# Graph network over 128 graphs: x turned by DMA and VectorE, the odd-weight check on other engines, and a new order of steps

## The chip, the cores and the metric

The kernel runs on one core of one Trainium2 chip. A core has five engines that run their own instruction streams in order and wait for each other by semaphores: TensorE (PE; its weight loads are shown apart as PEld), VectorE (DVE), ScalarE (ACT), GpSimd (POOL) and SyncE (SP), which issues nearly all DMAs of this kernel. The metric is the device time of one execution in microseconds; the profile shows one execution of the program.

## The reference

There are 128 graphs of 64 nodes with 128 features (x), and a 0/1 adjacency matrix for each (adj), symmetric and with ones on the diagonal; about an eighth of the entries are ones. For each pair of nodes a message is computed and the messages of the neighbours are added up:

```python
pair_feats = concatenate([f_i, f_j], axis=-1)
messages = _mlp(pair_feats, msg_w0, ...) * coupling_matrix[..., None]
agg = sum(messages, axis=2)
updated = part_feats + _mlp(concatenate([part_feats, agg], axis=-1), upd_w0, ...)
# _mlp: relu(x @ w0 + b0), layer norm, relu(h @ w1 + b1), layer norm, h @ w2 + b2
```

All of it is float32.

## The kernel before, in words

The kernel computes messages for existing edges alone. Graphs go in pairs (64 pairs, one graph on partitions 0 to 63 and one on 64 to 127), four pairs make a block (`PB = 4`, 16 blocks, `NB`), and each graph has room for `CAP = 640` edges, so a pair has 10 tiles of 128 edges, and a chunk is four tiles: 160 chunks, ten to a block.

For each block, ahead of its chunks: `load_adj` and `load_x` bring the adjacency (`an`, 128 KB) and x (`xn`, 256 KB) by SP's queue. `rank` (L729) is a VectorE scan along the adjacency's rows that numbers each row's edges; `count` (L738) is a small matmul, and `place` and `place_out` on GpSimd turn the counts into edge positions (`posall`). `odd_weights` (L805) checks on VectorE that every adjacency entry is 0 or 1: it forms (a - 1) * a and takes the largest absolute value into `nball`. At the very end `flag_in` reads `nball`; if anything is odd, a dense path computes everything instead. With these inputs it is not taken. `turn_x` (L813) transposes the block's four 128x128 tiles of x on TensorE into a PSUM bank (`ma`), and `turn_x_out` (L819) copies them to `xnT` on ScalarE. `rows_both` multiplies `xnT` by the two halves of w0; `rows_hi` and `rows_lo` split the products into a high and a low part (`abh`, `abl`) in the type that `gather` multiplies.

For each pair: `distance` (ScalarE) and `make_tp` (VectorE) build a 0/1 matrix `tp` that says which edge slot belongs to which row node; `node_rows` casts it to `i` on GpSimd, `marks` (TensorE) and `compare` (VectorE) make `j` for the column node, and `stack` copies parts of both into `S` by SP's DMAs (`s<-i`, `s<-j`). `node_marks` turns `tp` by a DMA transpose (`oh`).

For each chunk: `gather` multiplies S by abl and abh into PSUM (`hps`), `relu0` (ScalarE) makes `h`, `turn_h` transposes it on TensorE into the one `hT` bank so that `stats0` (VectorE) can take the layer norm's statistics, `layer1` multiplies h by w1 (`z`), `relu1` (ScalarE or VectorE) makes `y`, and `stats1` takes its statistics. `weights` (GpSimd) and `reduce` (TensorE) add the messages up, and a `Unit` of steps per block runs the update network and ends in `finish`, four VectorE operations and the DMA to the output.

What sets the order is a list: each step is entered by `at(n, tag, fn, ...)` with a number of the chunk and gets the time `144 * n + t`, where `t` comes from the table `WHEN`, by the step's name and its place. The steps are then sorted by this time and emitted one after another, which gives each engine's order. The scheduler of the framework is off in this part (`manual_schedule`); it only adds the semaphores. A step's number is a rank in a list and no time on the chip.

`keep_busy` is filler: matmuls of constants whose results nobody reads, at the start.

Of the kernel before, what the change touches and what calls it, by code (L numbers as in the profile page):

```python
# [49 lines left out]
    "count": {8: -202, 101: 130, 102: 110, 115: -196},  # L50
    "count.0": {100: 66},
    "count_out": {9: -224, 101: 56, 102: 96, 115: -273},
    "count_out.0": {100: 79},
    "degrees": {9: -369, 101: -144, 102: -4, 115: -419},
    "degrees.0": {100: 58},
    "distance": {0: -532, 3: 185, 5: -470, 8: -359, 103: 34, 104: 302, 105: -163, 106: 312,
        107: -610, 108: 189, 158: -893, 159: -639, 160: -591, 161: -589, 162: 13, 163: -1137},
    "distance.0": {100: 163},
    "distance.1": {101: 208},
    "distance.2": {102: 283},  # L60
    "empties.0": {100: 156},
    "empties.1": {100: 154},
    "empties.10": {100: -158},
    "empties.11": {100: 84},
# [42 lines left out]
    "inverse_of": {0: -218, 5: 125, 125: -319, 126: -100, 127: 107, 128: 421, 129: 168, 130: 263,  # L107
# [1549 lines left out]
```

## Time and profile before

| | |
|---|---|
| time, median of 3 runs | 496.4 us (495.78 to 496.48) |
| span of the profiled execution | 495.0 us |
| TensorE busy | 484.8 us (98%) |
| VectorE busy | 462.3 us (93%) |
| ScalarE busy | 397.9 us (80%) |
| GpSimd busy | 353.0 us (71%) |
| mean busy share of the DMA engines on SP's queue | 60.4% |

A busy time is the union of an engine's instructions. Matmul ends are modelled, so distances between starts tell more of TensorE than lengths. In a list of groups, each row has the line, the engine, the operation, what it writes and reads, the count, then the total busy time, the mean of one in ns, and the idle time before it. Rows of a timeline start with the start and the length in microseconds.

### The profile page before, as it was taken

To read this page: it belongs to the slowest core of one execution; us is meant where nothing else is said; L and a number is where in the kernel's file an instruction comes from. 1 tells how busy PE (TensorE), PEld (TensorE's weight loads), DVE (VectorE), ACT (ScalarE), POOL (GpSimd) and SP (SyncE) were. 2 spreads that over 40 slices of the span, in tenths; PEclk is the share of its full clock that TensorE was granted. 3 is DMA by queue.
4 is the path that set the end of the run, shared out by engine and by line. 5 is a ranking of instruction groups with operands and counts; after the bars stand their busy time and mean duration, and the time that the engine had idled before them with its cause. 6 is when DMAs were issued, how large, how long until landed. Compare 5 with 4: busy or idle time off the path is not lost.

```text
span 495.0 us, 15915 instructions
## 1 busy us (share of the span) xinstructions
PE 484.8 (98%) x5947; PEld 461.3 (93%) x5947; DVE 462.3 (93%) x1225; ACT 397.9 (80%) x907; POOL 353.0 (71%) x563
## 2 busy tenths in 40 slices
PE   7999999999999999999999999999999999999994
PEld 5798999999999999999999999999999999999994
DVE  7989989999999999999999999999999999989975
ACT  7999978888787887878878787887878778767753
POOL 3276768878778787777779777787877678576661
PEclk9999999999999999999999999999999999999998
DMA  4676685667656575765757657466956775564311
GB/s 123 140 176 150 135 142 120 129 139 152 143 121 140 117 155 130 154 137 114 147 109 164 130 134 158 110 139 130 170 126 115 161 102 132 134 102 107 61 39 47
DMA packets 91474, 63.55 MB, mean 128 GB/s; under 512 B 57473, under 2 KB 75522, under 8 KB 91394
## 3 DMA queue, kind: packets, MB, share of 16 engines
q1 hardware_dynamic: 91106, 62.36, 60.4%
q8 instruction: 49, 0.80, 0.7%
q14 instruction: 31, 0.25, 0.1%
q10 hardware_dynamic: 288, 0.13, 0.1%
HBM read 7.15 MB, written 4.19 MB: 23 GB/s over the span
## 4 chain that ended last, share of the span: by engine, by line


## 5 line engine op out<-in xcount | busy, mean ns | idle before, releaser
L984 PE MATMUL z<-w1c,h 128*128 128x128 f32 x1280 | 190.0, 275 | 0.0
L984 PEld LDWEIGHTS z<-w1c,h 128*128 128x128 f32 x1280 | 171.7, 191 | 3.9 <-issue 0.4
L936 ACT ACTIVATE h<-hps,b0c 128x512 f32<-128x512 f32 x160 | 109.0, 681 | 42.3 <-PE hps L931 40.7
L627 DVE BATCH_NORM_STATS2 st<-hT 128x6 f32<-128x256 f32 x320 | 122.2, 418 | 15.3 <-PE hT L941 12.7
L627 DVE BATCH_NORM_STATS2 st<-y 128x6 f32<-128x256 f32 x320 | 125.3, 419 | 0.0
L978 ACT ACTIVATE z<-b1b,m_sd 128x128 f32<-128x128 f32 x320 | 118.4, 371 | 6.5
L941 PE MATMUL hT<-ident,h 128*128 128x128 f32 x640 | 113.3, 276 | 0.2 <-DVE st L627 0.2
L931 PE MATMUL hps<-s,abl 128*128 128x512 f32 (+3 forms) x256 | 97.0, 381 | 0.6 <-DVE abl L865 0.3
L971 POOL TENSOR_TENSOR u<-b1b,m_sd 128x512 f32<-128x512 f32 x80 | 87.5, 1103 | 7.8 <-ACT m_sd L635 7.7
L931 PE MATMUL hps<-s,abh 128*128 128x512 f32 (+3 forms) x256 | 92.2, 365 | 0.0
L941 PEld LDWEIGHTS hT<-ident,h 128*128 128x128 f32 x640 | 77.2, 141 | 2.9 <-PE z L984 0.6
L1027 POOL TENSOR_TENSOR w<-oh,m_q 128x192 f32<-128x192 f16 x126 | 65.2, 533 | 17.2 <-DVE m_q L656 9.6
L914 DVE TENSOR_TENSOR j<-mk,cmpt 128x320 fp32r<-128x320 f32 x124 | 59.3, 478 | 2.8 <-PE mk L906 1.2
L995 ACT ACTIVATE y<-z 128x512 f32<-128x512 f32 x80 | 47.9, 598 | 17.3 <-PE z L984 17.0
L611 DVE CUSTOM_DVE_ANT_0 y<-z,u 128x512 f32<-128x512 f32 x80 | 54.2, 678 | 1.7 <-PE z L984 0.2
L931 PEld LDWEIGHTS hps<-s,abl 128*128 128x128 f32 x256 | 48.8, 191 | 5.2 <-ACT ab L851 2.0
L889 POOL CAST i<-tp 128x640 fp32r<-128x640 f16 x58 | 41.8, 721 | 16.6 <-DMA s<-i 11.5
L874 ACT ACTIVATE d<-slot,mid 128x640 f16<-128x640 f16 x64 | 52.4, 822 | 0.4 <-DVE tp L880 0.3
L931 PEld LDWEIGHTS hps<-s,abh 128*128 128x128 f32 x256 | 49.5, 193 | 0.2
L645 POOL TENSOR_TENSOR m_v<-m_v,st 128x20 f32<-128x20 f32 x31 | 7.2, 232 | 57.5 <-DVE st L627 54.6
L1042 PE MATMUL ys<-y,w 128*32 128x128 f32 x1488 | 44.1, 274 | 0.0
L1042 PEld LDWEIGHTS ys<-y,w 128*32 128x32 f32 x1488 | 39.6, 110 | 2.6 <-issue 1.7
(193 smaller groups left out, 883.2 us busy)
## 6 DMA issues: line engine op xcount, KB each, us to landing
s<-j SPq DMA_DIRECT2D x124, 160.0 KB, 2.8
s<-i SPq DMA_DIRECT2D x124, 160.0 KB, 2.7
xn<-in_x_dram SPq DMA_DIRECT2D x15, 256.0 KB, 3.6
out_dram<-uo SPq DMA_DIRECT2D x15, 256.0 KB, 2.5
an<-in_adj_dram SPq DMA_DIRECT2D x16, 128.0 KB, 3.9
oh<-tp SPq DMA_TRANSPOSE x64, 3.5
xn<-in_x_dram SPq DMA_DIRECT2D x2, 128.0 KB, 2.9
out_dram<-uo SPq DMA_DIRECT2D x2, 128.0 KB, 3.9
```

Of the source, the lines that this page charges most:

```text
L611: nc.vector._custom_dve(TENSOR_ADD_SAT, out=o, in0=ps, in1=sb, s0=BIG, s1=0.0)
L627: nc.vector.bn_stats(st, src.rearrange("p t c -> p c t"))
L874: nc.scalar.activation(D[p], slot, AF.Abs, bias=blocks[b]["mid"][:, q:q + 1], scale=-1.0)
L914: nc.vector.tensor_tensor(JR[p][:, c], MK.pop((p, k))[:, 0:HC], cmpt[:, c], op=ALU.is_equal)
L931: nc.tensor.matmul(HP[n][:, c:c + w], lhsT=blocks[g // (2 * PB)]["ab", g // 4 % 2][k][:, g % 4, :], rhs=S[g // 2][:, g % 2, e:e + w], star ...
L936: nc.scalar.activation(H[n], HP.pop(n), AF.Relu, bias=b0c)
L941: nc.tensor.transpose(HT[n][:, t, :], H[n][:, t * P:(t + 1) * P], ident)
L971: nc.gpsimd.tensor_tensor(U[n], bc(W["b1b"], CH), SR[q][:, k:k + CH].unsqueeze(2).to_broadcast([P, CH, C]), op=ALU.mult)
L978: nc.scalar.activation(z_of(n)[:, t, :], W["b1b"], AF.Copy, scale=SR[q][:, k:k + 1])
L984: nc.tensor.matmul(ps[:, t, :], lhsT=H[n][:, t * P:(t + 1) * P], rhs=W["w1c"], start=by_vector(n) and t == 0, stop=True, skip_group_check= ...
L1027: (nc.vector if p == NP - 2 else nc.gpsimd).tensor_tensor(WT[p][:, g], oh, qs, op=ALU.mult)
L1042: nc.tensor.matmul(YS[b][g * N + m * HN:g * N + (m + 1) * HN, k, :], lhsT=w[:, g, m, u, :], rhs=y, start=(u == 0), stop=(u == TH - 1), til ...
```

## The change

It does four things.

1. For blocks 2 to 15, x is loaded a second time, straight from HBM, by four DMAs on SP's queue (`load_xt`). Each writes 32 partitions. Partition 32c + b gets, for every 32-row group k of the block's 512 rows, the 32 numbers of row 32k + b and columns 32c to 32c + 31, a run of 128 bytes. VectorE's transpose, which turns each 32x32 square of its input by itself, then gives `xnT` at once (`swap_x`). The four TensorE transposes and ScalarE's copy of these blocks go. Blocks 0 and 1 stay as they were. The first load of x stays too, for the residual.
2. `odd_weights` computes a - 1 and then (a - 1) * a on GpSimd, and a new step `odd_sum` lets ScalarE add up the absolute values of the row. The sum is compared with 0 as the maximum was.
3. `WHEN` is replaced as a whole, so all steps stand in a new order.
4. Some small things follow from the order: tiles are no longer dropped from the tables by the step that happened to come last, and `S`, `usdb` and the statistics are made by whichever step comes first.

```diff
-    "load_adj": {1: -901, 102: -1519, 103: 320},
-    "rank": {6: -172, 101: 62, 102: -12},
-    "turn_x": {6: -532, 101: -146, 115: -480},
+    "load_adj": {1: 1034, 102: 1731, 103: 755},
+    "load_xt": {2: 613, 102: 827, 115: 1278},
+    "rank": {6: 397, 101: -593, 102: 1209},
+    "swap_x": {7: 256, 115: 2738},
+    "turn_x": {101: 1025},
...
+        def load_xt(b):
+
+            xp = blocks[b]["xp"] = blkp.tile([P, PB * P // 32, 32], F32, name="xp", bufs=1)
+            rows = xf[b * PB * P:(b + 1) * PB * P, :].rearrange("(k b) c -> b k c", b=32)
+            for c in range(C // 32):
+                nc.sync.dma_start(xp[c * 32:(c + 1) * 32], rows[:, :, c * 32:(c + 1) * 32])
+
+        def swap_x(b):
+
+            blk = blocks[b]
+            blk["xnT"] = blkp.tile([P, PB * P], F32, name="xnT", bufs=4)
+            nc.vector.transpose(blk["xnT"], blk.pop("xp").rearrange("p k a -> p (k a)"))
...
         def odd_weights(b):
 
             an = blocks[b]["an"]
-            a2 = adp.tile([P, PB, N], F32, name="a2")
-            nc.vector.scalar_tensor_tensor(a2, an, 1.0, an, op0=ALU.subtract, op1=ALU.mult)
-            nc.vector.tensor_reduce(nball[:, b:b + 1], a2.rearrange("p q j -> p (q j)"),
-                                    axis=AX.X, op=ALU.max, apply_absolute_value=True)
+            a2 = blocks[b]["a2"] = adp.tile([P, PB, N], F32, name="a2", bufs=1)
+            nc.gpsimd.tensor_scalar(a2, an, 1.0, None, op0=ALU.subtract)
+            nc.gpsimd.tensor_tensor(a2, a2, an, op=ALU.mult)
+
+        def odd_sum(b):
+
+            a2 = blocks[b].pop("a2").rearrange("p q j -> p (q j)")
+            nc.scalar.activation(a2, a2, AF.Abs, accum_out=nball[:, b:b + 1])
...
                 at(max(o - 7, 13), "", odd_weights, b)
-                at(o - 4, "", turn_x, b)
-                at(o - 3, "", turn_x_out, b)
+                at(o - 6 if b > 1 else 5, "", odd_sum, b)
+                if b == 1:
+                    at(o - 4, "", turn_x, b)
+                    at(o - 3, "", turn_x_out, b)
+                else:
+                    at(o - 8, "", load_xt, b)
+                    at(o - 3, "", swap_x, b)
```

Line numbers of the changed kernel are higher by 58 to 79 than those of the kernel before, so that L817 (the transposes of x) is L892 there, L729 (the scan) is L800 and so on.

Three places show what the order does. The first is TensorE in the middle of the program, where a block's x was turned (`xn` to `ma`), before:

```order
L941 MATMUL hT<-ident,h 128x128 x2
L984 MATMUL z_2798<-w1c,h 128x128 x2
L906 LDWEIGHTS posall
L906 MATMUL mk<-tp,posall 128x320
L984 MATMUL z_2798<-w1c,h 128x128 x2
L817 MATMUL ma<-ident,xn 128x128 x4
L906 LDWEIGHTS posall
```

These four transposes stand nowhere on TensorE in the changed program; the row `STREAM_TRANSPOSE xnT<-xp` on VectorE, below, has taken their place.

The second is SP's queue and VectorE around the load of the adjacency (`an`) of block 6. SP before (`s<-` are the stacks, `oh` the DMA transposes of tp):

```order
L896 DMA s<-i_1570 64x640
L1016 DMA_TRANSPOSE oh<-tp 128x5x128
L896 DMA s<-j_1732 64x640
L717 DMA an<-in_adj_dram 128x4x64
L896 DMA s<-j_1732 64x640
```

SP in the changed program:

```order
L1085 DMA_TRANSPOSE oh<-tp 128x5x128
L789 DMA xp<-in_x_dram 32x16x32 x4
L1230 DMA out_dram<-uo 128x4x128
L971 DMA s<-j_2124 64x640 x2
L775 DMA an<-in_adj_dram 128x4x64
L971 DMA s<-i_2275 64x640
```

VectorE in the changed program, from finish (`uo`) to the scan (`rk`) that reads this load:

```order
L1227 SCALAR_TENSOR_TENSOR uo<-mu,um_q,xo 128x128 x4
L714 RECIPROCAL m_q<-m_sq 128x20
L685 BN_STATS st_2080<-hT 128x6 x2
L669 ISA y<-z_2262,u 128x512
L987 TENSOR_TENSOR j_2288<-mk,cmpt 128x320
L955 TENSOR_SCALAR tp<-d,deg 128x640
L685 BN_STATS st_2317<-hT 128x6 x2
L685 BN_STATS st_2245<-y 128x6
L987 TENSOR_TENSOR j_2288<-mk,cmpt 128x320
L669 ISA uy<-mu,usdb 128x512
L800 SCALAR_TENSOR_TENSOR rk<-first,an 128x256
L795 STREAM_TRANSPOSE xnT<-xp 128x512
```

Before, 290 steps of the sorted list lay between the load of block 6 and its scan. Now there are 18, and the load stands in SP's queue behind the output's DMA of an earlier block, which reads what finish writes.

The third is the start, on VectorE, before (`a` and `nball` are the check, `cumall` to `mid` the first block's places, `s<-mk` and `s<-z` the first compares, `abl` the low part for the first gather):

```order
L729 SCALAR_TENSOR_TENSOR rk<-first,an 128x256
L809 SCALAR_TENSOR_TENSOR a_215<-an 128x256
L810 TENSOR_REDUCE nball<-a_215 128x1
L747 TENSOR_SCALAR cumall<-raw 128x4
L782 TENSOR_TENSOR before<-cumall,rk 128x4
```
```order
L880 TENSOR_SCALAR tp<-d,deg 128x640
L1351 TENSOR_TENSOR s<-mk,cmpt 64x320
L1351 TENSOR_TENSOR s<-z_250,cmpt 64x320
L1351 TENSOR_TENSOR s<-mk,cmpt 64x320
L1351 TENSOR_TENSOR s<-z_250,cmpt 64x320
L865 TENSOR_TENSOR abl<-mu,abh 128x256
```

And in the changed program:

```order
L800 SCALAR_TENSOR_TENSOR rk<-first,an 128x256
L818 TENSOR_SCALAR cumall<-raw 128x4
L853 TENSOR_TENSOR before<-cumall,rk 128x4
L855 TENSOR_TENSOR mid<-cumall,before 128x4
L861 SCALAR_TENSOR_TENSOR posall<-rk,before,an 64x64 x2
L800 SCALAR_TENSOR_TENSOR rk<-first,an 128x256
L955 TENSOR_SCALAR tp<-d,deg 128x640 x2
L940 TENSOR_TENSOR abl<-mu,abh 128x256
L1431 TENSOR_TENSOR s<-mk,cmpt 64x320
L1431 TENSOR_TENSOR s<-z_263,cmpt 64x320
```

The check is gone from here, both tp and the first abl now stand ahead of the compares, and on TensorE two filler groups instead of three stand ahead of the first count matmul.

More of the change, by code (lines that the diff above doesn't have):

```diff
@@ L53 @@
[L53 to L64, printed above, removed]
@@ new lines @@
+    "ahead.1": {100: 205},
+    "ahead.10": {100: 1443},
+    "ahead.11": {100: 1474},
+    "ahead.2": {100: 1088},
+    "ahead.5": {100: 1450},
+    "ahead.8": {100: 1701},
+    "ahead.9": {100: 1642},
+    "bias0": {3: 1200, 112: 2460, 113: -3698, 114: 3910},
+    "bias0_0": {115: 6744},
+    "bias0_2": {115: 5813},
+    "bounds": {100: -14487},
+    "compare.0": {
+        0: 1091, 2: 1187, 5: 1081, 7: 997, 102: 1226, 103: 1565, 104: 1351, 105: 1243, 106:
+        1195, 107: 1166, 158: 2883, 159: 3321, 160: 4008, 161: 4190, 162: 4930, 163: 5108},
@@ new lines @@
+    "compare.1": {
+        1: 1098, 3: 1195, 6: 1037, 8: 1085, 102: 1394, 103: 1509, 104: 1314, 105: 1297, 106:
+        1152, 107: 1103, 157: 1251, 158: 3034, 159: 3663, 160: 4113, 161: 4757, 162: 4957, 163:
+        5363},
+    "compare_here.0.0": {100: 739},
+    "compare_here.0.1": {100: 860},
+    "compare_here.1.0": {101: 1170},
+    "compare_here.1.1": {101: 1184},
+    "count": {8: 693, 101: 620, 102: 1434, 115: 744},
+    "count.0": {100: -1424},
+    "count_out": {9: 695, 101: 971, 102: 1330, 115: 751},
@@ new lines @@
+    "count_out.0": {100: -1325},
+    "degrees": {9: 706, 101: 278, 102: 897, 115: 1493},
+    "degrees.0": {100: -2451},
+    "distance": {
+        0: 316, 3: 996, 5: 545, 8: 420, 103: 970, 104: 1527, 105: 1062, 106: 1062, 107: 1072,
+        108: 970, 158: -239, 159: 421, 160: 2400, 161: 2718, 162: 3476, 163: 3255},
+    "distance.0": {100: -61},
+    "distance.1": {101: -239},
+    "distance.2": {102: 742},
+    "empties.0": {100: 1249},
+    "empties.1": {100: 1308},
+    "empties.10": {100: 1416},
@@ new lines @@
+    "empties.11": {100: 1438},
+    "empties.2": {100: 1077},
+    "empties.3": {100: 1296},
+    "empties.4": {100: 1219},
+    "empties.5": {100: 1236},
+    "empties.6": {100: 1020},
+    "empties.7": {100: 1046},
+    "empties.8": {100: 1506},
+    "empties.9": {100: 1659},
+    "finish": {8: 1260, 110: 3288, 111: 5703, 112: 6182, 113: 5589, 114: 8453},
+    "finish_0": {115: 11035},
+    "finish_2": {115: 11129},
+    "flag_in": {100: 5046},
+    "flag_max": {100: 5327},
+    "flag_out": {100: 6053},
@@ new lines @@
+    "odd_sum": {4: 844, 101: 1436, 115: 846},
+    "odd_sum.0": {100: -2094},
+    "odd_weights": {3: -149, 101: -1366, 102: 950, 115: 193},
+    "odd_weights.0": {100: -2035},
+    "ones": {100: 12228},
+    "place": {1: 732, 101: 1105, 102: 1121, 115: 2317},
+    "place_first": {100: -1013},
+    "place_out": {3: 803, 101: 1116, 102: 1068, 115: 2242},
+    "place_pair.0": {100: -586},
+    "place_rest": {100: 181},
+    "rank": {6: 397, 101: -593, 102: 1209},
+    "rank.0": {100: -3707},
+    "reduce.-1": {163: 6177},
@@ new lines @@
+    "root_of": {
+        1: 898, 6: 1026, 100: 1598, 101: 1128, 127: 2711, 128: 4118, 129: 4909, 130: 5350, 131:
+        6052},
+    "rows.0": {101: 1094},
+    "rows.0.0.0.2": {100: -183},
+    "rows.0.0.2.4": {100: 600},
+    "rows.1": {100: 874, 101: 926},
+    "rows_both": {8: 294, 114: 288, 115: 3901},
[28 rows of a table added]
+    "seed_all": {
[47 rows of a table added]
+    "sums_out": {4: 908, 112: 2874, 113: 5315, 114: 5379},
+    "sums_out_0": {115: 5710},
+    "sums_out_2": {115: 6267},
+    "swap_x": {7: 256, 115: 2738},
[44 rows of a table added]
+    "turn_out.uh": {1: 791, 111: 2541, 112: 5413, 113: 6077, 114: 6131},
@@ L822, in turn_x_out @@
                 blk["xnT"] = blkp.tile([P, PB * P], F32, name="xnT", bufs=4)
[L823 removed]
+            nc.scalar.copy(blk["xnT"][:, q0 * P:q1 * P], blk.pop(("x_ps", q0))[:, q0 * P:q1 * P])
         def rows(b, half, k0=0, k1=4):
@@ L843, in rows_hi @@
             blk = blocks[b]
-            if k0 == 0:
+            if ("ab", half) not in blk:
                 blk["ab", half] = [blkp.tile([P, 4, C], F32R, name=v, bufs=3)
@@ L1362, in turn_x_out_rest @@
         def turn_x_out_rest():
-            nc.scalar.copy(blocks[0]["xnT"][:, 2 * P:PB * P], blocks[0].pop("x_ps")[:, 2 * P:])
+            nc.scalar.copy(blocks[0]["xnT"][:, 2 * P:PB * P], blocks[0].pop(("x_ps", 2))[:, 2 * P:])
         early(".0", rank, 0)
```

237 lines of the change are left out of this document (103 added, 134 removed), and 440 rows, old and new, of the table WHEN.

## The prediction

> **What bounds the kernel now.** I read the page's busy times first, then the busy times of each engine by stretch, then the waits of TensorE alone. The page's chain of work is empty here, so the bound is read from the stretches. The span of the profiled execution is 495.0 us, 1.4 us under the median of the three runs (496.4), and I carry that difference over at the end.
>
> ```profile
> PE 484.8 (98%) x5947; PEld 461.3 (93%) x5947; DVE 462.3 (93%) x1225; ACT 397.9 (80%) x907; POOL 353.0 (71%) x563
> ```
> ```profile
> 0.00:12.00 12.00, 8.97 (x59) 6.14 (x59) 8.96 (x25) 8.35 (x16) 4.27 (x15) 1.00 0.49 125
> 179.33:208.66 29.33, 29.33 (x379) 28.40 (x374) 28.08 (x75) 23.95 (x55) 22.72 (x36) 1.00 0.65 136
> 50.00:400.00 350.00, 350.00 (x4407) 337.99 (x4406) 336.52 (x880) 287.44 (x649) 271.48 (x424) 1.00 0.66 137
> 485.00:495.00 10.00, 3.71 (x27) 2.83 (x25) 4.48 (x18) 2.72 (x10) 0.58 (x3) 0.77 0.21 58
> ```
> ```profile
> PE ys L1334 <- DVE first L519: 1.9, 1, 1.9
> PE mk L906 <- DVE tp L880: 0.8, 1, 0.8
> PE hT L941 <- DVE st L627: 0.2, 1, 0.2
> ```
>
> The columns of the stretches are length, then busy time of PE, PEld, DVE, ACT and POOL. TensorE is busy for 350.00 of 350 us at full clock, and the waits charged to it are few and lie at the start. So between the first and the last few microseconds the time is the length of TensorE's own stream, and only what shortens that stream, or tears a hole in it, counts. VectorE is the next engine: 28.08 of 29.33 us, the length of one block of four graph pairs, as these two rows show (the little count matmul stands once in each block):
>
> ```profile
> 196.93 0.17 PE L738 MATMUL ma<-rk,lt 128*128 128x4 f16 x1
> 226.26 0.17 PE L738 MATMUL ma<-rk,lt 128*128 128x4 f16 x1
> ```
>
> **Removed from TensorE.** Fourteen blocks lose four transposes each. What they cost is the distance between the starts of what stands before and after them, not the modelled length:
>
> ```profile
> 205.15 0.61 PE L984 MATMUL z<-w1c,h 128*128 128x128 f32 x4
> 205.59 0.60 PE L817 MATMUL ma<-ident,xn 128*128 128x128 f32 x4
> 206.03 0.30 PE L906 MATMUL mk<-tp,posall 128*128 128x320 f16 x1
> ```
> ```profile
> L817 PE MATMUL ma<-ident,xn 128*128 128x128 f32 x62 | 9.4, 273 | 0.0
> ```
>
> From 205.59 to 206.03 is 0.44 us, so the block shrinks from 29.33 to 28.89 us and the whole by 14 x 0.44 = 6.2 us. The other TensorE instructions are the same in number and shape, only in another order. The busy time charged to all 62 transposes, 9.4 us, x 56/62 = 8.5 us is the upper bound; the distance of starts is the truer price.
>
> **VectorE.** These rows price what leaves, and the neighbours of what comes:
>
> ```profile
> L809 DVE SCALAR_TENSOR_TENSOR a<-an 128x256 f32<-128x256 f32 x16 | 12.7, 795 | 0.0
> L810 DVE TENSOR_REDUCE nball<-a 128x1 f32<-128x256 f32 x16 | 6.7, 420 | 0.6
> L865 DVE TENSOR_TENSOR abl<-mu,abh 128x512 fp32r<-128x512 f32 (+1 forms) x17 | 10.9, 641 | 0.0
> L611 DVE CUSTOM_DVE_ANT_0 y<-z,u 128x512 f32<-128x512 f32 x80 | 54.2, 678 | 1.7 <-PE z L984 0.2
> L880 DVE TENSOR_SCALAR tp<-d,deg 128x640 f16<-128x640 f16 x64 | 29.7, 465 | 0.1
> ```
>
> The check leaves with 795 + 420 ns a block. The 32x32 transpose of 128x512 is not in the trace. Its bounds are the fastest row here for its elements, 465 ns for 640 two-byte ones, and two passes of the slowest 128x512 row, 2 x 678 = 1356 ns. I take 0.65, since the 512-element rows lie at 641 and 678. VectorE's work per block becomes 28.08 - 1.22 + 0.65 = 27.5 us, or 28.2 at the upper bound, against a block of 28.89. A price is also on a page of the Trainium skill: "Vector Engine (DVE) Microarchitecture Reference", on the reshape front-end, says that the transpose sustains one element per cycle per lane; at 0.96 GHz ("VectorE: DVE Perf Modes", Specifications) that is an estimate of 0.53 us and a fixed part, with which VectorE's sum would stay about where I have it, and no run here shows it yet.
>
> **ScalarE and GpSimd.** ScalarE loses the copy of the turned x and gains an Abs pass of half the width. GpSimd gains two passes over 128x256.
>
> ```profile
> L823 ACT COPY xnT<-ma 128x512 f32<-128x512 f32 x15 | 8.7, 581 | 1.4 <-PE ma L817 1.3
> L1097 ACT COPY uyT<-hps 128x256 f32<-128x256 f32 x1 | 0.4, 373 | 0.5 <-PE hps L1092 0.5
> L861 POOL CAST abh<-ab 128x512 fp32r<-128x512 f32 x15 | 9.3, 622 | 0.0
> L765 POOL TENSOR_TENSOR pos<-rk,before 128x256 f32<-128x256 f16 x15 | 9.2, 612 | 0.0
> ```
>
> The Abs costs between 373 ns (same width, no sum) and 581 ns (twice the width): ScalarE stays at 24 of 28.89 us. GpSimd's pair costs between 0.31 + 0.61 and 2 x 0.61 = 1.2 us: 22.72 + 1.2 = 23.9 of 28.89. Neither is near the block's length, and TensorE's stream hides both. If that cover were gone, ScalarE's part would be worth -0.2 to 0 and GpSimd's 1.2 us a block.
>
> **The second load of x.** Each block adds four DMAs on SP's queue and 256 KB in 2048 runs of 128 bytes.
>
> ```profile
> q1 hardware_dynamic: 91106, 62.36, 60.4%
> s<-j SPq DMA_DIRECT2D x124, 160.0 KB, 2.8
> xn<-in_x_dram SPq DMA_DIRECT2D x15, 256.0 KB, 3.6
> an<-in_adj_dram SPq DMA_DIRECT2D x16, 128.0 KB, 3.9
> ```
> ```profile
> 202.38 0.39 SPq L1160 DMA_DIRECT2D out_dram<-uo  x1
> 202.84 0.50 SPq L896 DMA_DIRECT2D s<-j  x1
> 203.39 1.29 SPq L1016 DMA_TRANSPOSE oh<-tp  x1
> ```
>
> SP's pitch is 202.84 - 202.38 = 0.46 to 203.39 - 202.84 = 0.55 us a plain issue, so four issues take some 2.2 us of SP. What they take of the DMA engines is bounded by bytes below (0.26 of 62.36 MB of 0.604 x 495 us: 1.3 us of all 16) and by the mean packet above (2048 of 91106: 6.7 us). From 0.65 of a block's DMA time that goes to between 0.69 and 0.88. A 256 KB load in long runs lands after 3.6 us; with 6.7 us added it is 10 us at worst. The rows of x need the turned x only after VectorE's transpose, and in the changed order SP has issued the load before the output's DMA, behind which it waits. I take no cost.
>
> **The wait that the new order adds.** The adjacency's load stood far ahead of the rank scan that reads it. Now SP issues it behind the output's DMA, which waits for VectorE's finish, and behind two s<-j. From the end of finish it lands after 0.46 + 2 x 0.55 + 3.9 = 5.5 us. The first row below says that SP does stand there for VectorE's finish (uo) today, 14 times. VectorE has between finish and scan one reciprocal, five statistics, y, two compares, tp and uy (taken at y's price):
>
> ```profile
> SPq L1160 <- DVE uo L1157: 20.4, 14, 3.5
> ```
> ```profile
> L656 DVE RECIPROCAL m_q<-m_sq 128x20 f32<-128x20 f32 x32 | 8.5, 266 | 0.6 <-ACT m_sq L651 0.6
> L627 DVE BATCH_NORM_STATS2 st<-y 128x6 f32<-128x256 f32 x320 | 125.3, 419 | 0.0
> L914 DVE TENSOR_TENSOR j<-mk,cmpt 128x320 fp32r<-128x320 f32 x124 | 59.3, 478 | 2.8 <-PE mk L906 1.2
> 213.86 0.76 DVE L627 BATCH_NORM_STATS2 st<-hT 128x6 f32<-128x256 f32 x2 [0.87 <-PE hT L941]
> ```
>
> That is 0.27 + 5 x 0.42 + 2 x 0.68 + 2 x 0.48 + 0.47 = 5.1 us by means, less where neighbours overlap. So the scan waits 0.4 us a block, perhaps 1.1, and behind it queue the transpose of x, tp, statistics of y and then the statistics of hT, for which TensorE's next transposes into the one hT bank wait. VectorE's demand with the wait is 27.9 to 28.6 us of 28.89, and it now idles in such places anyway (0.87 us in the last row, just behind the scan). I take nothing of it for TensorE; the bound is the whole 1.1 us in 13 blocks.
>
> **The start.** In the first 12 us TensorE has 8.97 us of work, most of it filler.
>
> ```profile
> 3.39 0.69 DVE L729 TENSOR_TENSOR_SCAN rk<-first,an 128x256 f16<-128x256 f32 x1 [1.54 <-DMA an<-in_adj_dram]
> 4.62 0.21 PE L738 MATMUL ma<-rk,lt 128*128 128x4 f16 x1
> 9.87 0.49 DVE L1351 TENSOR_TENSOR s<-z,cmpt 64x320 fp32r<-64x320 f32 x1
> 10.39 0.42 DVE L865 TENSOR_TENSOR abl<-mu,abh 128x256 fp32r<-128x256 f32 x1
> ```
>
> The count matmul starts at 4.62 behind three filler groups though the scan is done at 4.08; the change puts two there, worth up to 0.5 us. The low part abl is taken before the four compares rather than after them, which lets the first gather go after two of them (2 x 0.49 us). VectorE's later compares limit the rest, so I take 0.6 us, with bounds 0 and 1.5. At the end the chain of the last block is the same instructions; I take 0, with 1 us either way.
>
> **Sum.** 495.0 - 6.2 - 0.6 = 488.2 us of span, and with the 1.4 us around it 489.6 us.
>
> **Rivals.**
> 1. The scan's wait replaces the gain (slower). For it: SP stands behind finish in every block and the margin is negative by the rows. Against: VectorE has 1.25 us idle a block. If the whole 1.1 us passes to TensorE, 489.6 + 13 x 1.1 = 504 us; it eats the gain of 6.8 from 0.52 us a block on. Chance 0.11, most of it near 499.
> 2. VectorE sets the block. With the transpose at 1.36 and the wait at 1.1 its block is 28.08 - 1.22 + 1.36 + 1.1 = 29.3 us, that of today: 495 to 497 us, no change. Chance 0.07.
> 3. The start and the end give more. With 1.5 us at the start and 1 us at the end: 487.7 us, and as little as 485.5 if the early blocks, where VectorE is full (rank and check in a row), gain as well. Chance 0.14.
> 4. The short runs clog the queues. At 6.7 us a block the stacks issued behind the load land late; if TensorE waits for what exceeds today's 3.6 us, that is 14 x 3.1 = 43 us, so 533 us. Against: the load's issue is followed by SP's wait for finish. Chance 0.03. "DMA: Bandwidth & Descriptors" (Specifications) of the Trainium skill speaks for this rival: under 512 bytes a transfer loses line rate to read-modify-write. By that rule the runs would cost near the upper bound; this trace cannot say, having no HBM run of 128 bytes.
>
> The forecast keeps 0.65. Its own range is 488 to 492. For 8 in 10 I take 485.5 to 497: it holds the forecast, rivals 2 and 3 and the mild part of 1. A difference of 0.2% (1 us) is about what a measurement of this kernel tells from none. Faster: 0.65 + 0.14 and part of 2 make 0.82; the same 0.06; slower 0.12.
>
> **What would show it.** Right: no TensorE waits worth a microsecond between 20 and 480 us, a distance of 28.9 us between count matmuls, a transpose near 0.65 us, and the last TensorE instruction about 6.5 us earlier. Wrong: a row in which VectorE's scan or TensorE's hT waits for the adjacency's DMA in each block by more than half a microsecond, a transpose above 1.3 us, or hps waiting for s<-j.

## The result: slower by 4.2%

The changed kernel takes 517.1 us (median of four runs, 516.2 to 518.5); the kernel before takes 496.1 us beside it. The ratio is 1.042, with an interval of 1.040 to 1.044. Forecast were 489.6 us and a range of 485.5 to 497. The profiled execution has a span of 515.9 us, 20.9 us more than before, at the same granted clock (0.995 before, 0.996 now).

The page of the changed kernel, busy times and the DMA queue:

```profile
PE 497.0 (96%) x5891; PEld 456.5 (88%) x5891; DVE 464.9 (90%) x1207; ACT 396.4 (77%) x925; POOL 377.5 (73%) x595
q1 hardware_dynamic: 120674, 66.03, 62.8%
```

TensorE has 56 instructions less, as the change says, and its busy time is longer; the lengths of its instructions are modelled, so waits hide in them. The waits of the same execution (total, times, longest):

```profile
PEld hT L1014 <- DVE st L685: 9.0, 17, 1.5
DVE rk L800 <- DMA an<-in_adj_dram: 6.5, 8, 1.7
PE hT L1014 <- DVE st L685: 6.0, 6, 1.3
```

TensorE's transposes of h now wait for VectorE's statistics (0.2 us before), and VectorE's scan waits for the adjacency's load. The groups that are new or have changed their length:

```profile
L987 DVE TENSOR_TENSOR j<-mk,cmpt 128x320 fp32r<-128x320 f32 x124 | 58.9, 475 | 4.9 <-PE mk L979 2.5
...
L955 DVE TENSOR_SCALAR tp<-d,deg 128x640 f16<-128x640 f16 x64 | 39.7, 622 | 0.4 <-ACT d L949 0.3
...
L800 DVE TENSOR_TENSOR_SCAN rk<-first,an 128x256 f16<-128x256 f32 x16 | 15.0, 938 | 6.5 <-DMA an<-in_adj_dram 6.5
...
L880 POOL TENSOR_SCALAR a<-an 128x256 f32<-128x256 f32 x16 | 14.0, 876 | 1.3 <-DMA an<-in_adj_dram 0.2
...
L881 POOL TENSOR_TENSOR a<-a,an 128x256 f32<-128x256 f32 x16 | 11.7, 731 | 1.3
...
L795 DVE STREAM_TRANSPOSE xnT<-xp 128x512 f32<-128x512 f32 x14 | 9.5, 682 | 0.0
```

VectorE lost 19.4 us of check and got 9.5 us of transposes. But its 64 tp, which nobody touched, went from 465 to 622 ns each (10.0 us more) and its 16 scans from 742 to 938 ns, while j stayed at its length (478 and 475 ns). So VectorE's sum is not smaller at all.

Where the 20.9 us lie can be read from the count matmul, which stands once in each block. Ten blocks of the changed kernel, and one short and two long ones among them (timeline, TensorE: start, length):

```profile
77.82 0.18 PE L809 MATMUL ma<-rk,lt 128*128 128x4 f16 x1
...
138.25 0.18 PE L809 MATMUL ma<-rk,lt 128*128 128x4 f16 x1
...
167.97 0.18 PE L809 MATMUL ma<-rk,lt 128*128 128x4 f16 x1
...
199.25 0.18 PE L809 MATMUL ma<-rk,lt 128*128 128x4 f16 x1
...
230.67 0.18 PE L809 MATMUL ma<-rk,lt 128*128 128x4 f16 x1
...
383.00 0.18 PE L809 MATMUL ma<-rk,lt 128*128 128x4 f16 x1
...
508.84 1.52 PE L1179 MATMUL z<-u2c,uyT 128*128 128x128 f32 x8
```

The same ten blocks before, and in both the last group of TensorE:

```profile
80.54 0.17 PE L738 MATMUL ma<-rk,lt 128*128 128x4 f16 x1
...
372.86 0.17 PE L738 MATMUL ma<-rk,lt 128*128 128x4 f16 x1
...
487.57 1.20 PE L1109 MATMUL z<-u2c,uyT 128*128 128x128 f32 x8
```

Ten blocks took 292.3 us and take 305.2: 12.9 us more. What lies ahead of them and behind them took 487.6 - 292.3 = 195.3 us and takes 508.8 - 305.2 = 203.6: 8.4 us more. And the blocks come in two lengths: 29.72 us (138.25 to 167.97) and 31.28 and 31.42 us (the two behind it), where the forecast had 28.89. In all, the five long ones take 31.24 to 31.42 us and four others 29.72 to 30.24; the first takes 29.19, where the same one took 28.42 before.

Why there are two lengths shows on VectorE and GpSimd at the scan. In the short block (changed kernel, timeline, these two engines alone):

```profile
154.95 0.68 DVE L800 TENSOR_TENSOR_SCAN rk<-first,an 128x256 f16<-128x256 f32 x1
154.97 0.96 POOL L1096 TENSOR_TENSOR w<-oh,m_q 128x192 f32<-128x192 f16 x1
...
155.90 1.03 POOL L1042 TENSOR_TENSOR u<-b1b,m_sd 128x512 f32<-128x512 f32 x1
156.16 0.95 DVE L955 TENSOR_SCALAR tp<-d,deg 128x640 f16<-128x640 f16 x1
```

And in the block of 31.42 us, with a tp and a w just ahead of the place, and the transpose of TensorE that ends up waiting:

```profile
213.67 0.38 DVE L955 TENSOR_SCALAR tp<-d,deg 128x640 f16<-128x640 f16 x1
...
215.97 0.51 POOL L1096 TENSOR_TENSOR w<-oh,m_q 128x192 f32<-128x192 f16 x1
216.44 1.04 POOL L1042 TENSOR_TENSOR u<-b1b,m_sd 128x512 f32<-128x512 f32 x1
216.79 1.23 DVE L800 TENSOR_TENSOR_SCAN rk<-first,an 128x256 f16<-128x256 f32 x1 [0.76 <-DMA an<-in_adj_dram]
217.42 1.11 POOL L964 CAST i<-tp 128x640 fp32r<-128x640 f16 x1
...
218.56 1.16 DVE L955 TENSOR_SCALAR tp<-d,deg 128x640 f16<-128x640 f16 x1
...
223.12 0.44 PE L1014 MATMUL hT<-ident,h 128*128 128x128 f32 x2 [0.90 <-DVE st L685]
```

In the short block the scan comes first and takes 0.68 us; GpSimd's w, begun 0.02 us after it, takes 0.96 us in place of 0.51 (215.97). In the long one the adjacency is 0.76 us late, GpSimd's u (the product of a bias that VectorE's y adds) has begun, and the scan takes 1.23 us: its own 0.68 and the rest of u. The tp behind it takes 1.16 us, where the one of the short block, behind another u, takes 0.95, and one with no GpSimd operation in its way 0.38 (213.67). So 0.76 us of lateness become some 1.5 us on VectorE against the short block (0.76 + 0.55 + 0.21), and 0.8 to 1.5 us of waiting on TensorE. All five long blocks have both, a scan that waits 0.54 to 0.79 us for the adjacency and behind it a wait of hT for the statistics; no block below 30 us has a scan that waits.

The Trainium skill, "SBUF — State Buffer", section "Who interferes with whom", says that VectorE and GpSimd share one pair of ports, that a VectorE instruction with two inputs in SBUF, or a tensor_scalar in a two-port mode, needs it, and that whoever comes second waits until the first has finished. The trace agrees: the scan (two inputs in SBUF) and tp wait a GpSimd operation out, and j, with one input in PSUM, does not (475 ns here, 478 before).

### The profile page after: what moved, and what is told of

Read it like the earlier page. It is cut to its first block, busy times and chain, and to the rows that moved or that the text cites. A ratio compares the mean times of both kernels' runs of the same rounds, so it can differ in the third digit from the quotient of the medians.

```text
span 515.9 us, 15894 instructions
## 1 busy us (share of the span) xinstructions
PE 497.0 (96%) x5891; PEld 456.5 (88%) x5891; DVE 464.9 (90%) x1207; ACT 396.4 (77%) x925; POOL 377.5 (73%) x595
## 3 DMA queue, kind: packets, MB, share of 16 engines
q1 hardware_dynamic: 120674, 66.03, 62.8%
## 4 chain that ended last, share of the span: by engine, by line
PE 69%; DVE 10%; ACT 6%; DMA 5%; POOL 5%; issue 3%; SPq 1%; DVEq 0%; POOLq 0%
PE z L1055 21%; PE hps L1004 12%; PE hT L1014 11%; PE mu L1179 8%; DVE st L685 6%; PE ys L1111 4%; PE ma L1162 3%; PE mk L979 3%; DMA an<-in_adj_dram 2%; PE mu L907 2%; ACT h L1009 2%; DMA oh<-tp 2%; ACT z L1049 1%; PE ma L907 1%; POOL w L1096 1%
## 5 line engine op out<-in xcount | busy, mean ns | idle before, releaser
L1055 PE MATMUL z<-w1c,h 128*128 128x128 f32 x1280 | 182.0, 277 | 0.3
L1055 PEld LDWEIGHTS z<-w1c,h 128*128 128x128 f32 x1280 | 162.8, 192 | 4.5 <-ACT z L1049 1.8
L685 DVE BATCH_NORM_STATS2 st<-hT 128x6 f32<-128x256 f32 x320 | 123.6, 416 | 14.6 <-PE hT L1014 13.2
L1014 PE MATMUL hT<-ident,h 128*128 128x128 f32 x640 | 123.5, 277 | 6.1 <-DVE st L685 6.0
L685 DVE BATCH_NORM_STATS2 st<-y 128x6 f32<-128x256 f32 x320 | 123.2, 416 | 1.4 <-ACT y L1064 0.8
L1004 PE MATMUL hps<-s,abl 128*128 128x512 f32 (+3 forms) x256 | 98.3, 387 | 2.6 <-POOL before L832 1.2
L1042 POOL TENSOR_TENSOR u<-b1b,m_sd 128x512 f32<-128x512 f32 x80 | 83.3, 1048 | 22.3 <-ACT m_sd L693 9.5
L1014 PEld LDWEIGHTS hT<-ident,h 128*128 128x128 f32 x640 | 79.5, 141 | 20.8 <-DVE st L685 9.0
L1096 POOL TENSOR_TENSOR w<-oh,m_q 128x192 f32<-128x192 f16 x126 | 65.6, 538 | 12.9 <-DVE m_q L714 8.5
L964 POOL CAST i<-tp 128x640 fp32r<-128x640 f16 x58 | 44.2, 765 | 8.5 <-DMA s<-i 6.3
```

Source lines behind the costliest of these rows:

```text
L685: nc.vector.bn_stats(st, src.rearrange("p t c -> p c t"))
L1004: nc.tensor.matmul(HP[n][:, c:c + w], lhsT=blocks[g // (2 * PB)]["ab", g // 4 % 2][k][:, g % 4, :], rhs=S[g // 2][:, g % 2, e:e + w], star ...
L1014: nc.tensor.transpose(HT[n][:, t, :], H[n][:, t * P:(t + 1) * P], ident)
L1042: nc.gpsimd.tensor_tensor(U[n], bc(W["b1b"], CH), SR[q][:, k:k + CH].unsqueeze(2).to_broadcast([P, CH, C]), op=ALU.mult)
L1055: nc.tensor.matmul(ps[:, t, :], lhsT=H[n][:, t * P:(t + 1) * P], rhs=W["w1c"], start=by_vector(n) and t == 0, stop=True, skip_group_check= ...
L1096: (nc.vector if p == NP - 2 else nc.gpsimd).tensor_tensor(WT[p][:, g], oh, qs, op=ALU.mult)
```

## The experiments

Three theories were set against each other at first: the new **operations** cost the time, the new **order** does, or, as a part of the order, the **late load** of the adjacency. "The old order" is the table of the kernel before with the new steps at the places of the old ones. Times are medians; the kernel before lies at 495.8 to 496.1 us beside them.

| kernel | us | ratio to before |
|---|---|---|
| changed kernel | 517.1 | 1.040 to 1.044 |
| x1 old order, all new operations | 498.9 | 1.0035 to 1.0069 |
| x2 new order, old operations | 526.9 | 1.057 to 1.064 |
| x3 new order, adjacency early | 512.0 | 1.030 to 1.036 |
| x9 the same for blocks 2 and 3 too | 511.5 | 1.028 to 1.038 |
| x4 new order, check on VectorE | 525.9 | 1.055 to 1.061 |
| x13 x9 without the check | 510.2 | 1.025 to 1.029 |
| x16 x9 without GpSimd's u | 517.1 | 1.040 to 1.043 |
| x17 before, without GpSimd's u | 496.4 | 1.0000 to 1.0018 |
| x18 x9 without VectorE's transpose | 512.4 | 1.030 to 1.035 |
| x5 old order, VectorE's transposes only | 496.7 | 0.9998 to 1.0019 |
| x6 old order, check on GpSimd only | 498.2 | 1.0028 to 1.0056 |
| x10 before, TensorE's transposes left out | 494.8 | 0.9959 to 0.9985 |
| x10b before, TensorE's transposes twice | 506.3 | 1.018 to 1.022 |
| x11 x5 with the seeds sooner | 496.1 | 0.9991 to 1.0011 |
| x12 x5 with mk later | 496.2 | 0.9996 to 1.0014 |
| x14 x12 with the second load sooner | 494.5 | 0.9952 to 0.9978 |
| x8 x1 with the check moved | 498.0 | 1.0025 to 1.0054 |
| x19 all new operations, three places mended | 495.3 | 0.9981 to 1.0000 |

### Operations or order

x1 is the changed kernel with the table of the kernel before, and these entries for the new steps:

```diff
+    "load_xt": {2: -700, 102: -120, 115: -1028},
+    "swap_x": {7: -640, 115: -668},
+    "odd_sum": {4: -130, 101: -100, 115: -530},
+    "odd_sum.0": {100: -1313},
```

> The table of the kernel before sets the order again, with all the new operations in it: the four 128-byte-run loads ahead of where the TensorE transposes stood, VectorE's transpose in their place, the check on GpSimd and ScalarE at the old check's place. If the new ORDER is what costs, this is the forecast's own kernel without it: 487 to 493 us, blocks of about 28.9 us on TensorE. If the new OPERATIONS cost (GpSimd's 1.6 us more per block, VectorE's transpose, the fourfold load), it stays above 500 us. If the LATE LOAD of the adjacency alone costs, it is below 496 too, since the load stands a whole block ahead of the scan in this order; it does not tell that from the order at large.

x2 is the changed kernel's table with the old steps:

```diff
-                    at(o - 8, "", load_xt, b)
-                    at(o - 3, "", swap_x, b)
+                at(o - 4, "", turn_x, b)
+                at(o - 3, "", turn_x_out, b)
...
-            nc.gpsimd.tensor_scalar(a2, an, 1.0, None, op0=ALU.subtract)
-            nc.gpsimd.tensor_tensor(a2, a2, an, op=ALU.mult)
+            nc.vector.scalar_tensor_tensor(a2, an, 1.0, an, op0=ALU.subtract, op1=ALU.mult)
+            nc.vector.tensor_reduce(nball[:, b:b + 1], a2.rearrange("p q j -> p (q j)"),
+                                    axis=AX.X, op=ALU.max, apply_absolute_value=True)
```

> The table of the changed kernel with the old operations: x is turned by TensorE and copied by ScalarE (at the list places next to VectorE's transpose), the check is two VectorE operations, the second load is gone. ORDER or LATE LOAD: as slow as the changed kernel or slower, 515 to 530 us (TensorE has its 0.44 us per block back, VectorE 0.5 us more per block than with the transpose). OPERATIONS: back to about 496 to 500 us.

With the new operations the order alone makes 517.12 - 498.86 = 18.3 us, with the old ones 30.8 us. In the new order the new operations even help by 9.8 us; in the old one they cost 2.7 us. So the order is the cause of most of the loss, but x1 lies neither where "order" nor where "operations" had it: the gain did not come even in the old order. Both questions go on below.

### The late load

x3 changes one number, x9 three:

```diff
-    "load_adj": {1: 1034, 102: 1731, 103: 755},
+    "load_adj": {1: -332, 102: 1731, 103: 755},     (x3)
+    "load_adj": {1: -332, 102: -1000, 103: 100},    (x9)
```

> The changed kernel with one number of its table changed: the adjacency load of blocks 4 to 15 is issued about one block earlier, as far ahead of the scan as in the kernel before. LATE LOAD: the six to seven blocks of 30.2 to 31.4 us fall to the 29.75 us of the others, so 9 to 10 us go: 506 to 510 us, and no scan waits for a DMA or runs longer than 0.7 us. ORDER (the rest of it): the remaining 10 us over the kernel before stay, so not below 504 us. OPERATIONS, or a load that is only a witness: 515 to 518 us.

> The changed kernel with the adjacency loads of blocks 4 to 15 a block earlier, and those of blocks 2 and 3 earlier too. If the 3 us that the new order loses up to 52 us of the span come from the late loads of blocks 2 and 3: 508 to 511 us. If they come from the order of the first blocks at large: 511 to 514 us, like the run with blocks 4 to 15 alone.

x3 takes 5.1 us away, less than the 9 to 10 us expected of the late load. The waits of hT for VectorE and the scan's own length fall, in x9 (groups):

```profile
L1014 PE MATMUL hT<-ident,h 128*128 128x128 f32 x640 | 123.0, 276 | 1.3 <-DVE st L685 1.0
...
L800 DVE TENSOR_TENSOR_SCAN rk<-first,an 128x256 f16<-128x256 f32 x16 | 12.1, 755 | 1.8 <-DMA an<-in_adj_dram 1.7
```

x9's further 0.5 us cannot be told from nothing. The ten blocks of x9, and a short one among them:

```profile
77.63 0.18 PE L809 MATMUL ma<-rk,lt 128*128 128x4 f16 x1
...
286.31 0.18 PE L809 MATMUL ma<-rk,lt 128*128 128x4 f16 x1
...
316.05 0.18 PE L809 MATMUL ma<-rk,lt 128*128 128x4 f16 x1
...
376.47 0.18 PE L809 MATMUL ma<-rk,lt 128*128 128x4 f16 x1
...
502.73 1.52 PE L1179 MATMUL z<-u2c,uyT 128*128 128x128 f32 x8
```

They take 298.8 us: of the 12.9 us lost in these blocks 6.3 are gone and 6.5 stay; start and end take 203.9 us, as in the changed kernel (203.6). The short block is as long as that of the changed kernel, 29.74 us for 29.72. So the late load is a quarter of the loss, not half of it as expected, and tp is as long as ever (629 ns).

### The check on GpSimd

x4 puts it back on VectorE in the new order; x6 puts only it on GpSimd in the old one; x13 is x9 without it in blocks 2 to 15. (x4 has the lower half of the diff of x2, from `odd_weights` on, and no step `odd_sum`; x6 has that half the other way round, in the kernel before, with the two `odd_sum` entries of x1.) x13:

```diff
         def odd_weights(b):
             an = blocks[b]["an"]
+            if b > 1:
+                return
```

> The changed kernel with the check back as two VectorE operations (1.2 us per block) at the list place of the GpSimd pair; GpSimd has 1.6 us and ScalarE 0.6 us per block less. OPERATIONS, if GpSimd's share of them costs (its long operations hold VectorE's scan and tp up): 505 to 512 us. ORDER or LATE LOAD: VectorE is late in this order already, so 517 to 530 us.

> The table of the kernel before, and of the new operations only the check on GpSimd and ScalarE; x is turned by TensorE as before. If the GpSimd pair pushes GpSimd's later operations onto VectorE's tp and scan, which then wait for them: 498 to 504 us. If the check is hidden, as the forecast had it: 494 to 497 us.

> The changed kernel with all adjacency loads early, as in the run before, and the odd-weight check left out in blocks 2 to 15 (no GpSimd pair, no ScalarE sum: an odd weight there would go unseen). If what is left of the loss (511.5 against 498.9 us for the same operations in the old order) is the order itself: 508 to 512 us. If in this order GpSimd's pair is what makes VectorE's tp wait, and with it TensorE: 499 to 506 us.

In the old order the check on GpSimd costs 2.1 us rather than nothing; its tp goes from 465 to 524 ns (x6, groups):

```profile
L899 DVE TENSOR_SCALAR tp<-d,deg 128x640 f16<-128x640 f16 x64 | 33.5, 524 | 0.6 <-ACT d L893 0.6
```

In the new order it is worth having: back on VectorE it costs 8.8 us more. Without any check 510.2 us remain, 1.3 us under x9 and within the spread of the two, so the check is not what the rest is made of.

### Who sets the block in the new order

x16 leaves GpSimd's 80 products u out, x17 is the same in the kernel before, x18 leaves VectorE's transpose out. x16 and x18 build on x9:

```diff
-            U[n] = up.tile([P, CH, C], F32, name="u")
-            nc.gpsimd.tensor_tensor(...)
+            U[n] = uc                 # a constant tile (x16, x17)
...
-            nc.vector.transpose(blk["xnT"], blk.pop("xp").rearrange("p k a -> p (k a)"))
+            blk["xnT"] = xc           # a constant tile (x18)
```

> The changed kernel with all adjacency loads early (511.45 us), and GpSimd's 80 products u left out (VectorE's y adds a constant in their place, so the result is not the reference's). The u are the GpSimd operations that VectorE's tp most often waits out. If these waits make what is left of the loss: 498 to 505 us. If the new order loses it at TensorE's own hand-offs: 507 to 511 us.

> Control: the kernel before with the same 80 products u left out. Its tp waits little (465 ns on average against 370 alone), so both theories expect 493 to 497 us; what it gains here is to be taken off what the new order gains.

> The changed kernel with all adjacency loads early (511.45 us), and VectorE's transpose left out (its 14 x 0.68 us; the products read a constant in place of x turned, so the result is not the reference's; the second load still runs). The run without u showed VectorE's scan 0.8 us longer and each block 0.57 us longer, so VectorE is the late one right there. If VectorE's path through that place sets the block of the new order: 0.4 to 0.68 us less per block, 502 to 506 us. If TensorE's own hand-offs set it and VectorE has slack in this direction: 509 to 511.5 us.

x16 went where neither theory had it: with 83 us of GpSimd work less the program is 5.6 us **slower**. Its timeline shows why, GpSimd and VectorE at the scan:

```profile
217.42 1.04 POOL L1149 TENSOR_TENSOR m<-c2u,deg 128x512 f32<-128x512 f32 x1
217.53 1.47 DVE L802 TENSOR_TENSOR_SCAN rk<-first,an 128x256 f16<-128x256 f32 x1
```

GpSimd begins m, another of its products, 0.11 us before the scan, and ten of the 16 scans take 1.47 to 1.50 us. The blocks go from 29.74 to 30.32 us:

```profile
200.76 0.18 PE L811 MATMUL ma<-rk,lt 128*128 128x4 f16 x1
...
231.08 0.18 PE L811 MATMUL ma<-rk,lt 128*128 128x4 f16 x1
```

That shows VectorE and GpSimd waiting for one another at work, and lengthening a block. It does not say whether such waits make the remaining loss, because they did not become less: against x9 the tp fall from 629 to 518 ns on the mean, 7.1 us for 64, but the scans rise from 755 to 1244 ns, 7.8 us for 16. x18 takes 0.68 us off VectorE at the same place, and the blocks keep their length (259.09 to 288.81, 29.72 us); as a whole it takes 512.4 us, just above the 509 to 511.5 expected and not told from x9:

```profile
259.09 0.18 PE L810 MATMUL ma<-rk,lt 128*128 128x4 f16 x1
...
288.81 0.18 PE L810 MATMUL ma<-rk,lt 128*128 128x4 f16 x1
```

So 29.72 to 29.75 us is the length of the shortest regular blocks of the new order, whether the load is early (x3, x9), the check is gone (x13) or VectorE lacks the transpose (x18); only the first of the ten is shorter, 29.2 us in each of them. Neither the late load nor GpSimd's check nor VectorE's transpose sets that length. Whether GpSimd's other operations do, by holding up tp, no run tests. In the short block of x9 shown above (286.31 to 316.05) the longest waits charged to TensorE's two streams are single ones of 0.2 us.

What speaks for TensorE itself, the way in which its own instructions follow one another with small waits, is only that the trace names nothing larger. That is argued and not shown, and whether ScalarE's hand-offs have a part was not settled.

### Why the gain did not come in the old order

x5 is the old order with the transposes on VectorE and the check left on VectorE. x10 takes the kernel before and leaves TensorE's transposes out, x10b issues them twice:

```diff
         def turn_x(b, q0=0, q1=PB, bank=abank):
+            if b > 1: return                                    (x10)
-            for q in range(q0, q1):
+            for q in [q for q in range(q0, q1) for _ in range(2 if b > 1 else 1)]:   (x10b)
```

> The table of the kernel before, and of the new operations only the second load and VectorE's transpose; the check stays on VectorE. If the transposes' 0.44 us per block on TensorE are worth what the forecast said and the old order with all new operations lost it to the check on GpSimd: 488 to 493 us. If VectorE's 0.68 us per block or the four more DMAs cost it: 496 to 502 us.

> The kernel before with TensorE's four transposes of x left out in blocks 2 to 15 (ScalarE copies x itself, so what TensorE then multiplies is not the turned x); nothing is put in their place. If TensorE's stream is the bound, as the forecast had it: 14 x 0.44 us less, 489 to 491 us. If the transposes filled a wait for ScalarE's last seed of z, which is read from the run with VectorE's transposes alone (TensorE waits 0.30 us there in each block): most of it comes back as that wait, 494 to 496.5 us.

> The kernel before with each of TensorE's transposes of x in blocks 2 to 15 issued twice. TensorE has no gap left at that place, so both theories expect the whole 14 x 0.44 us on top: 501 to 503 us. Below 499 us would say that the place has slack in this direction as well, and that neither theory holds.

x10 has nothing in place of the transposes and gains 1.3 us of 6.2. Its usual block is 29.21 us, 0.12 shorter, not 0.44:

```profile
195.97 0.17 PE L738 MATMUL ma<-rk,lt 128*128 128x4 f16 x1
...
225.18 0.17 PE L738 MATMUL ma<-rk,lt 128*128 128x4 f16 x1
```

So the transposes stood where TensorE would have waited anyway. x5 has the same 29.21 us in its usual block, so VectorE's transposes and the four loads cost such a block nothing. The other direction is not symmetric: the second set costs 10.2 us, 0.73 us for each 0.44 and more than the 501 to 503 us that both theories expected, and VectorE's scans go from 742 to 1107 ns with it. What TensorE waits for shows in x5 (timeline, TensorE and VectorE where they stood):

```profile
206.57 0.49 DVE L927 TENSOR_TENSOR j<-mk,cmpt 128x320 fp32r<-128x320 f32 x1
...
207.12 0.30 PE L919 MATMUL mk<-tp,posall 128*128 128x320 f16 x1
...
207.19 0.52 PEld L995 LDWEIGHTS z<-w1c,h 128*128 128x128 f32 x4 [0.38 <-ACT z L989]
```

There are two candidates. The profile charges 0.38 us to ScalarE's seeds of z (the bias that ScalarE writes into z before `layer1` adds its products). But mk has one bank of PSUM, j reads it from 206.57 to 207.06, and the next mk starts at 207.12. x10 has the same hole, mk again 0.06 us behind the end of j:

```profile
204.37 0.49 DVE L917 TENSOR_TENSOR j<-mk,cmpt 128x320 fp32r<-128x320 f32 x1
...
204.92 0.30 PE L909 MATMUL mk<-tp,posall 128*128 128x320 f16 x1
```

And the kernel before has the limit in its own trace, next to the transposes that the prediction shows:

```profile
205.35 0.49 DVE L914 TENSOR_TENSOR j<-mk,cmpt 128x320 fp32r<-128x320 f32 x1
```

j ends there at 205.84, so with the same 0.06 us the mk at 206.03 could have come 0.13 us earlier and no more, whatever was taken out ahead of it: an estimate from these rows, and the block shrank by 0.12. To tell the two candidates apart, x11 moves a ScalarE operation from ahead of the seeds to behind them; x12 puts the second mk behind the four z:

```diff
-    "upd_root0": {9: 115, ...      "upd_shift": {9: 201, ...
+    "upd_root0": {9: 340, ...      "upd_shift": {9: 460, ...      (x11; its load_xt 2: -900)
-    "marks.0": {0: -68, 2: 80, ...
+    "marks.0": {0: -68, 2: 99, ...                                (x12, x14)
-    "load_xt": {2: -700, ...
+    "load_xt": {2: -900, ...                                      (x14)
```

> The old order with VectorE's transposes, check on VectorE, and three numbers of the table changed: ScalarE's um_sd (0.28 us) and GpSimd's usdb that reads it stand behind ScalarE's five seeds of z in place of ahead of them, and the second load is issued a little earlier. If ScalarE's seeds set the pace where the transposes stood: they come 0.23 us sooner per block, 2 to 3 us less than the run with VectorE's transposes alone, and up to 1.4 us more if block 3's wait for a stack goes: 492 to 495 us. If they do not: 496 to 498 us.

> The run with VectorE's transposes alone (old order, check on VectorE; 496.65 us), with one number of the table changed: in each block the one product mk whose place came right after TensorE's transposes of x now comes after the four z products that followed it. If TensorE's 0.30 us of wait there is for the one PSUM bank of mk, which VectorE's j has to read before the next mk may write it: the four z fill that wait, 10 to 13 blocks x 0.30 us less, 492.5 to 494.5 us. If the wait has another cause, it moves along: 496 to 497.5 us.

> The same, and the second load issued 200 units of the list (some 4 us) earlier, as in the run with the seeds sooner, where it took block 3 from 28.89 to 27.14 us. If the bank of mk is the cause and block 3's wait adds to it: 491 to 493.5 us, faster than both kernels. If the bank is not the cause: 495 to 496 us.

With the seeds sooner the wait stays at 0.30 us in each block (29.21 to 29.25 us in most), so the seeds are not it, whatever the row says, and that x10 came out in the range set for them (494 to 496.5) was right by the wait and not by its cause. With mk behind the z the wait is gone (x14, timeline):

```profile
204.01 0.30 PE L919 MATMUL mk<-tp,posall 128*128 128x320 f16 x1
204.15 1.24 PE L995 MATMUL z<-w1c,h 128*128 128x128 f32 x8
...
205.23 0.30 PE L919 MATMUL mk<-tp,posall 128*128 128x320 f16 x1
```

The bank of mk is the cause of that wait; but at most half of its 0.30 us comes out as shorter blocks (29.04 to 29.15 us in five of nine of x14; the others take 29.3 to 29.5), since 0.2 to 0.4 us come back in some blocks, around a gather or the products with w0 behind it. x12 as a whole is not told from the kernel before: my 492.5 to 494.5 was too low, and it is its trace, not its time, that speaks for the bank. x14 also sends the four loads of the second x off earlier. In block 3 they had held up a stack on SP's queue (the next s<-i is issued at 53.51 us in x5 and at 50.49 in the kernel before), and TensorE's gather waited 1.2 us (x5, timeline):

```profile
57.18 0.47 PE L944 MATMUL hps<-s,abl 128*128 128x512 f32 x1 [1.19 <-POOL i L904]
```

Block 3 takes 28.5 us in x12 and 27.0 us in x14. x14 is faster than both kernels, if by less than the 491 to 493.5 us expected: 494.5 us, 0.22 to 0.48% under the kernel before.

### All operations, mended

x8 is x1 with the check pair where GpSimd otherwise waits for VectorE; x19 has the check there and the two changes of x14:

```diff
-    "odd_weights": {3: -40, ...
+    "odd_weights": {3: -742, ...
```

> The old order with all new operations, and one number changed: the GpSimd pair of the check stands some 10 us earlier in each block, ahead of an m_v for which GpSimd waits 2.1 us, where it pushes nothing back. If it was the pushed-back GpSimd operations that held VectorE's tp (1.24 us in place of 0.38 in eight blocks): the tp is short again and 488 to 493 us. If the loss of the old order with the new operations lies elsewhere: 497 to 500 us.

> All operations of the change in the old order with the three places mended that the runs named: the mk behind the four z, the second load 200 units earlier, and GpSimd's check pair in GpSimd's idle time (ScalarE's sum in place of its copy of x). If the order alone stood between the new operations and a gain: as fast as the run with the first two mended and the check on VectorE, 493.5 to 495.5 us. If GpSimd's pair costs wherever it stands: 496 to 498.5 us.

In x8 the third tp of a block falls from 1.24 to 0.75 us, but the block stays at 29.2 us, with the wait for mk's bank in it (its mk too starts 0.41 us behind the start of the last z, where 0.11 is usual): 498.0 us, not the 488 to 493 expected. x19 has both and takes 495.3 us, inside its expectation. Its usual block takes 29.06 us. So the whole change can be had without loss, and with mk moved as well it is worth at most 1 us here, against the 6.8 of the forecast. What moving mk alone would do in the kernel before was not run.

## Why the prediction was wrong, step by step

**"From 205.59 to 206.03 is 0.44 us, so the block shrinks from 29.33 to 28.89 us."** This step failed, and it failed without the new order: x10 leaves just these transposes out and the block becomes 29.21 us. A stretch without idle time shows that the engine is never seen waiting, not that its work sets the time. Behind the transposes stood a limit 0.12 us away: the one bank of mk (x5, x10, x12), which the second mk may not write before VectorE's j has read the first. The distance of starts priced the instruction rightly and the gain wrongly.

**"The other TensorE instructions are the same in number and shape, only in another order."** The second failed step, and the larger one. I took the order as free. x1 against the changed kernel prices it at 18.3 us. The late load is 5.1 us of it (x3). Of the rest, in the profiled executions, 6.5 us lie in the ten blocks (299.2 us in x3, 292.7 in x1) and 5 to 6 us at the start and the end. For this rest the cause stays open.

**The added wait.** Here the mechanism was right and the size was not. I had the scan wait 0.4 us a block, perhaps 1.1; it waits 8 times. The longest, 1.7 us, is at the very start, where it also stood before; the seven others are of 0.2 to 1.1 us, 4.8 us in all. The step that failed is "I take nothing of it for TensorE". My rival 1 priced it at one for one. In fact a scan that is late meets GpSimd's u and waits again, the tp behind it waits too, and TensorE's hT waits 0.8 to 1.5 us.

**VectorE.** The transpose was 0.682 us for 0.65: right. The sum of 27.5 us a block left out that tp and the scan have no fixed length. The estimate of 0.53 us and a fixed part, from the Trainium skill, "Vector Engine (DVE) Microarchitecture Reference", on the reshape front-end, fits the run with a fixed part of 0.15 us.

**ScalarE and GpSimd.** GpSimd's pair took 0.88 + 0.73 = 1.61 us, above my 1.2. ScalarE's sum took 0.41 us and 0.19 more for reading its accumulator, 0.60 in all and just above my 0.58 (groups of the changed kernel):

```profile
L886 ACT ACTIVATE a<-a 128x256 f32<-128x256 f32 x16 | 6.5, 408 | 0.2 <-POOL a L881 0.2
```

"TensorE's stream hides both" was wrong for GpSimd: it costs 2.1 us in the old order (x6), where GpSimd has room for it but each tp of VectorE grows by 59 ns.

**The second load.** Its row among the DMA issues (times, size, us to landing):

```profile
xp<-in_x_dram SPq DMA_DIRECT2D x56, 64.0 KB, 2.6
```

It lands after 2.6 us, and the queue took 62.8% of the DMA engines for 60.4%, so rival 4 is dead. In time that is 0.628 x 515.9 - 0.604 x 495.0 = 25 us of all 16 engines, 1.8 us a block: near the bound by bytes (1.3) and far from that by packets (6.7). What the Trainium skill, "DMA: Bandwidth & Descriptors" (Specifications), says of transfers under 512 bytes does not show in the landing of these reads of 128-byte runs: the 64 KB loads land no later than those of the weights, 2.2 to 3.1 us. In the engines' time it could be there, as the 1.4 times that a byte of these runs cost against the mean byte before (25 us for 3.67 MB, 299 us for 62.36 MB). What I had at nothing and what did count once is SP's queue: in the old order the four issues delayed a stack by 3 us in one block (x5).

**Start and end.** I had 0.6 us of gain and 0. Together they lose 8.4 us, and early loads do not bring them back (x9). x1 loses 2.6 us of them too. By the starts of relu0's h at every tenth chunk, 4.2 us of the loss lie ahead of chunk 30 and 3.6 between chunks 130 and 140. The largest waits of TensorE there that the kernel before lacks are 0.7 us at 25.4 us (hT, for VectorE's statistics), 1.2 at 35.5 (a gather, for GpSimd's `before`) and 0.8 each at 436.4 and 439.5. They are under half of it; the rest, and their cause beyond the order, stay open.

**Rival 2**, VectorE as the bound, is refuted by x18 at the place of the transpose, in the new order. Of VectorE's other work no run says so.

## What to carry to other kernels

An engine that is busy throughout in a tightly packed program need not be the bound: ask for each gap that a removal would open what the next instruction behind it waits for, a buffer above all. Here one row of VectorE in the trace of the kernel before, j, would have given the answer. To leave the work out on the chip is a cheap test, and here it would have shown 1.3 us of the 6.2 hoped for. The order was worth more than the operations here, 18.3 us against 2.7: change the operations inside the old order first, and one place at a time.

## What the runs showed that I had not expected

- VectorE's scan and tp and GpSimd's operations exclude one another, and who begins first is decided by tenths of a microsecond: a scan takes 0.68 or 1.23 to 1.47 us, a tp 0.38 or up to 1.16 in the rows above. Taking 83 us of work from GpSimd made the program 5.6 us slower that way (x16), while it does nothing in the old order (x17).
- Two block lengths, 29.7 and 31.3 us, follow one another in one execution with the same instructions, and where the scan comes 0.76 us late it meets a GpSimd operation and loses 0.76 us more.
- Removing and adding are not symmetric: 0.44 us less on TensorE gave 0.12 us a block, 0.44 us more cost 0.73.
- A wait can be charged to an engine that had long been done: the profile named ScalarE's seeds for mk's wait, and only x11 and x12 told them apart.
